# A two-layer graph-attention kernel on one core: weighing in column tiles of 32, single weight sums, and another order of the first step's loads and casts

## The chip, the core and the metric

The kernel runs on one core of a Trainium2 chip. Its time is the device time of one execution in microseconds (us). A profiled execution of each kernel is there too; its span, from the first to the last instruction, is a little shorter than the time of a run. The engines are TensorE (PE, with its weight loads shown apart as PEld), VectorE (DVE), ScalarE (ACT), GpSimd (POOL) and SyncE (SP, which here only issues DMAs; a queue's issue of a DMA is shown as SPq or ACTq).

## What is computed

64 graphs of 256 nodes with 512 features go through two layers of masked attention. `adj` says for each graph which node may look at which.

```python
# layer 0: 4 heads of 64, layer 1: 8 heads of 64
h = maximum(layernorm(x), 0)
q, k, v = heads(h @ Wq), heads(h @ Wk), heads(h @ Wv)
sim = where(adj, q @ k.T / 8, -big)
x = x + (softmax(sim) @ v) @ Wo + bo
# layer 1: the same on the new x, with a second layernorm (gamma, beta) behind the
# maximum, w_qkv and w_out in place of the four weights, and the diagonal always allowed
```

All arithmetic is on 32-bit floats.

## The kernel before

Two graphs make a step (`G = 2`), so that there are 32 steps. Everything of a step lies in SBUF: 128 partitions, and 512 tokens in four tiles of 128 (`NT = 4`). The order of the instructions on PE, DVE, ACT and POOL is written out by hand: `at(period, place, fn, ...)` puts each piece of work into a list with a due place, `place` being counted from the start of a period of 6.13 places, and at the end the list is sorted and each piece issued. One period is one step of the pipeline: layer 1 of step s, with layer 0 of steps s+1 and s+2 between its pieces. The place decides the order of issue on every engine, and each engine works strictly in that order.

The dense products (projections `project_qk`, `project_v1`, and the output product `combine1`) are done with a scheme of seven block products in place of eight (`PRODUCT`); for it, sums and differences of blocks of the weights and of the activations are made beforehand. `weight_sums` makes the four for the weights, `act_sums0` and `act_sums1` those for the activations. A set of seven products (`at_set`) takes one place, each product a seventh. PSUM has four banks for them; the results are taken out by `evacuate` on DVE and ACT.

Between the sets stand the visits of the attention (`visit`), six in a period, each for a pair of heads in two graphs. A visit does, for the pair of the visit before, `weigh` (values times probabilities, L823), then the sums of the probabilities by a matmul with ones (L843), and then the `scores` of the next pair (L787). In `weigh`, po is a PSUM tile of 128 partitions: the first head of the pair writes partitions 0 to 63, the second 64 to 127. There are eight matmuls in a visit's `weigh`, each with a stationary operand of 128 x 64 and 256 moving columns; two of them, one for each head, stand in different columns of the array. The matmuls with ones have a stationary operand of 128 x 32, and four of them stand beside one another. The scores have 64 rows and 128 columns, two beside one another. Each of these 32-bit matmuls is two records in the trace.

Behind the matmuls of a visit, `invert` (DVE, L853) makes the reciprocals of the sums, eight small DMAs on SP spread them over the partitions (`invb`), and `normalise` (POOL, L870) multiplies the weighed values with them. The probabilities of the next pair go from the scores through `mask_scores` (DVE, L800), `exponentials` (ACT, L805) and `key_halves` (POOL, L813). In the first layer POOL also multiplies the queries of each pair by a row `ne` (L699, in `project_qk` after products 3 and 4); the scores of a pair wait for that.

Before the first period a prologue loads and prepares. SP issues the loads of x in four pieces and of the adjacency matrix (`load_h`); ACT's queue issues those of the first layer's weights and the biases (`first_weights`). POOL casts the adjacency matrix (`adjacency_cast`, L502), then makes the row scales of the first layernorm (`row_scales`, L548 to L552), with which ACT and DVE scale x (`scale_row`). PE then transposes x (L608). The weights of the second layer are transposed on PE in 16 blocks (`weight_block`, L461), in gaps of the prologue; then `second_sums` makes the four sums of each of q, k and v on DVE and of the output weights on POOL. The sixteen are issued in four groups of four, one group directly after another on its engine.

Of the kernel before, what the change touches and what calls it, by code (L numbers as in the profile page):

```python
# [13 lines left out]
ALU = mybir.AluOpType  # L14
# [301 lines left out]
def fast_path(  # L316
# [19 lines left out]
    nc = tc.nc  # L336
    P = 128
    B, N, D = x.shape
    DH = 64
    G = 2  # L340
    NSTEP = B // G
    NIC = N // P
# [20 lines left out]
    def mm_tile(shape, dt=FP, hold=False):  # L363
        tag = next(b for b in banks if b not in held)
        banks.remove(tag)
        banks.append(tag)
        if hold:
            held.add(tag)
        return ps_mm.tile(shape, dt, name="mm", tag=tag)
# [26 lines left out]
    B_OF = ((0, 8, 7), (1, 3, 1))  # L396
    PRODUCT = {1: (0, 0), 2: (1, 1), 3: (6, 2), 4: (3, 6), 5: (2, 3), 6: (4, 4), 7: (5, 5)}

    def weight_sums(eng, w):
        eng.tensor_tensor(w[:, 5], w[:, 0], w[:, 2], ALU.subtract)  # L400
        eng.tensor_tensor(w[:, 2], w[:, 2], w[:, 3], ALU.add)
        eng.tensor_tensor(w[:, 4], w[:, 2], w[:, 0], ALU.subtract)
        eng.tensor_tensor(w[:, 6], w[:, 1], w[:, 4], ALU.subtract)

    def act_sums0(b, eng=nc.gpsimd):
        eng.tensor_tensor(b[:, 3], b[:, 7], b[:, 0], ALU.subtract)
# [9 lines left out]
    wqk0 = const.tile([P, NB, HC, 2, H0], FP, name="wqk0")  # L416
    wv0 = const.tile([P, NC, I0], FP, name="wv0")
    wo0 = const.tile([P, PR0, D], FP, name="wo0")
    wqkv1 = const.tile([P, NB, HC, 3, H1], FP, name="wqkv1")
    wo1 = const.tile([P, NB, HP1, HD], FP, name="wo1")  # L420
# [4 lines left out]
    def first_weights():  # L425
        for i in range(2):
            for k, w in enumerate((wq, wk)):
                nc.scalar.dma_start(
                    wqk0[:, 2 * i:2 * i + 2, :, k, :].rearrange("p j c o -> p (j c) o"),
                    w[:, i * H0:(i + 1) * H0].rearrange("(c p) o -> p c o", p=P),  # L430
                )
        nc.scalar.dma_start(wv0, wv.rearrange("(c p) o -> p c o", p=P))
        nc.scalar.dma_start(wo0, wo.rearrange("(c p) o -> p c o", p=P))
        for v, t in ((bo, bo_b), (b_out, bout_b)):
            nc.scalar.dma_start(t, bass.AP(tensor=v.tensor, offset=v.offset, ap=[[0, P], [1, D]]))
        gbr = sm.tile([2 * NC, P], FP, name="gbr", tag="inv", bufs=1)
        nc.scalar.dma_start(gbr[:NC], gamma.rearrange("(c p) -> c p", p=P))
        nc.scalar.dma_start(gbr[NC:], beta.rearrange("(c p) -> c p", p=P))
        return gbr
# [18 lines left out]
    def weight_block(wr, n, c):  # L458
# [3 lines left out]
        for i in range(2):  # L462
# [1 line left out]
            dst = wqkv1[:, blk, c % HC, n, :] if n < 3 else wo1[:, blk, c % HC, :]  # L464
            copy = nc.vector.tensor_copy if i == 0 and c % 2 == 0 else nc.scalar.copy
            copy(dst, pw[:, i * H1:(i + 1) * H1])

    def second_sums(k):
        if k == 3:
            weight_sums(nc.gpsimd, wo1)  # L470
        else:
            weight_sums(nc.vector, wqkv1[:, :, :, k, :])


    S = [dict() for _ in range(NSTEP)]
# [339 lines left out]
    def weigh(s, lyr, pr, first):  # L815
        st = S[s]
        p, pd = st.pop(("p", lyr, pr))
        po = ps_sc.tile([P, G, N], FP, name="sc")
        for g in range(G):
            for kc in range(NIC):  # L820
                for e in range(2):
                    c0 = pr * P + e * DH
                    nc.tensor.matmul(  # L823
                        po[e * DH:(e + 1) * DH, g, :],
                        st[f"v{lyr}"][:, g * NIC + kc, c0:c0 + DH],
                        p[e][:, g, kc, :], start=(kc == 0), stop=(kc == NIC - 1),
                    )
        if lyr == 0:
            if first:
                st["oT0"] = act.tile([P, PR0, G, N], FP, name="oT0")  # L830
            dst = st["oT0"][:, pr]
        else:
            if first:
                st["oT1"] = act.tile([P, NB + 1, HP1, N], FP, name="oT1")
            b0, b1, step = B_OF[pr // HP1]
            dst = st["oT1"][:, b0:b1:step, pr % HP1, :]
        nc.scalar.copy(dst, po)  # L837

        sums = mm_tile([P, N])
        for g in range(G):  # L840
            for e in range(2):
                r0 = 32 * (2 * g + e)
                nc.tensor.matmul(  # L843
                    sums[r0:r0 + 32, :], ones, pd[:, e, g, :], start=True, stop=True
                )
        st["dst", lyr, pr] = dst, sums
# [33 lines left out]
    def at(period, place, fn, *args):  # L880
        events.append((period * PERIOD + place, len(events), fn, args))
# [14 lines left out]
    def visit(period, w, prev, cur):  # L896

        w -= 0.0003
        if 0 <= prev[0] < NSTEP:
            at(period, w, weigh, *prev)  # L900
            last = prev[:2] == (NSTEP - 1, 1)
            at(period, w + (0.05 if last and prev[2] in (1, 3) else 0), invert, *prev[:3])
            at(period, w + 0.55, normalise, *prev[:3])
        if 0 <= cur[0] < NSTEP:
            at(period, w, scores, *cur)
            at(period, w, mask_scores, *cur, 0)
            at(period, w + 0.05, exponentials, *cur, 0)
            at(period, w + 1 / 7, mask_scores, *cur, 1)
            at(period, w + 0.18, exponentials, *cur, 1)
            at(period, w + 0.2, key_halves, *cur, 0)  # L910
            at(period, w + 0.3, key_halves, *cur, 1)

    AT_C0, AT_Q0, AT_V0, AT_H1, AT_C1 = 3.0, 3.57, 4.57, 5.13, 5.131
    for s in range(-1, NSTEP):
        p = s
# [14 lines left out]
    for s in range(NSTEP):  # L930

        p = s - 2
        if s == 1:
            p -= 3.93 / PERIOD
        at(p - 1 if s != 1 else -2, 5.7 if s != 1 else 3.2, load_h, s)
        at(p, 0.2 if s != 1 else 2.4, adjacency_cast, s)
        for t in range(NT):
            at(p, 0.5 + 0.4 * t if s != 1 else 1.8 + 0.2 * t, norm0, s, t)
            at(p, 2.3 + 0.1 * t if s != 1 else 2.6 + 0.1 * t, scale_row, s, t)
        at(p, (3.146, 3.584)[s] if s < 2 else 2.2, adjacency_turn, s)  # L940
        at(p, (3.3, 3.727)[s] if s < 2 else 2.75, masks, s)
        for c in range(NC):
            at(p, AT_C0 + 0.14 * (c // 2) + 0.001 * c, transpose_h, s, 0, c)
        at(p, AT_C0 + 0.1, lambda s=s: act_sums0(S[s]["hT"]))
        at(p, AT_C0 + 0.2, lambda s=s: act_sums1(S[s]["hT"]))
        at_set(p, AT_Q0 if s != 1 else 3.3, SET, project_qk, s, 0, 0)
        for t in range(NT):
            at_dense(p, AT_V0 + 0.14 * t, 0.14, project_v0, s, t)
        p = s - 1
        if s == 0:  # L950
            p -= 2.23 / PERIOD
        at(p, 1.0 if s else 0.0, load_x, s)
        at(p, 1.8 if s else 0.8, first_bias, s)
        for t in range(NT):
            at_dense(p, AT_C0 + 0.01 + 0.14 * t, 0.14, combine0, s, t)
            at(p, AT_C0 + 0.3 + 0.14 * t, norm1, s, t)
            at(p, (3.55, 3.7, 4.05, 4.2)[t], norm1_rest, s, t)
            at(p, 3.62 + 0.08 * t, second_bias, s, t)
            at(p, 4.5 + 0.1 * t, scale_row, s, t)

        for c in range(NC):
            at(p, AT_H1 + 0.0001 * c, transpose_h, s, 1, c)
        at(p, AT_C1 + 0.15, lambda s=s: act_sums0(S[s]["hT"]))
        at(p, AT_C1 + 0.5, lambda s=s: act_sums1(S[s]["hT"]))
        p = s
        at_set(p, 0.0, SET, project_qk, s, 1, 0)
        at_set(p, 1.0, SET, project_v1, s)
        at_set(p, 2.0, SET, project_qk, s, 1, 1)
        at(p, 4.55, lambda s=s: act_sums0(S[s]["oT1"], engine_of(s, 1, 1)))
        if s < NSTEP - 1:  # L970
            at(p, AT_C1 + 0.1, lambda s=s: act_sums1(S[s]["oT1"]))
            at_set(p, AT_C1, SETC, combine1, s)
            at(p, 6.3, store, s)
        else:
            at(p, AT_C1 + 0.4, lambda s=s: act_sums1(S[s]["oT1"], nc.vector))
            at_set(p, AT_C1, (1, 5, 2, 3, 6, 7, 4), combine1, s)
            for n, (i, j) in enumerate(((0, 0), (0, 1), (1, 1), (1, 0))):
                at(p, AT_C1 + (3, 6, 6, 7)[n] / 7, store_block, s, i, j)

    gbr, blocks = [], []  # L980
    at(-3, 5.71, lambda: gbr.append(first_weights()))
    at(-2, 2.25, lambda: weight_sums(nc.vector, wqk0))
    at(-2, 3.5, lambda: blocks.extend(weight_loads()))
    at(-2, AT_V0 + 0.2, lambda: gamma_beta(gbr[0]))
    for i in range(16):
        place = 3.3 - 3.93 + 1 / 7 - 0.0005 if i < 4 else 0.2 + 0.07 * i if i < 8 else 1.34 + 0.1 * (i - 8)
        at(-1, place, lambda i=i: weight_block(blocks[i // 4], i // 4, i % 4))
    for k, place in enumerate((2.8, 2.85, 4.3, 4.5)):
        at(-1, place, second_sums, k)
    for _, _, fn, args in sorted(events, key=lambda e: e[:2]):  # L990
        fn(*args)

# [51 lines left out]
```

## Time and profile before

| | before |
|---|---|
| three runs, us | 3487.59, 3490.94, 3491.87 (median 3490.94) |
| profiled execution: time, span in us | 3486.23, 3484.4 |
| granted TensorE clock, mean | 0.996 |
| busy: PE, PEld | 3422.2 us (98%), 2635.1 us (76%) |
| busy: DVE, POOL, ACT | 1926.1 us (55%), 1922.1 us (55%), 1245.8 us (36%) |
| DMA | mean 48 GB/s |
| PE busy from 0 to 200 us, 200 to 3300, 3300 to 3485 | 164.28, 3094.66, 163.31 us |

A line of the list of groups gives the kernel line, engine, operation, the tiles written and read, the shapes and the number of instructions, then the busy time and the mean duration. A busy time is the time in which at least one instruction of the group was under way, so that matmuls that stand beside one another count once. In a timeline the first number is the start in us from the beginning of the span, the second the length of a merged stretch, xN the number of instructions in it, and the bracket the idle time before it and who ended it. The ends of matmuls are modelled: their starts are what can be read closely.

### The profile page before, as it was taken

To read this page: it belongs to the slowest core of one execution; us is meant where nothing else is said; L and a number is where in the kernel's file an instruction comes from. 1 tells how busy PE (TensorE), PEld (TensorE's weight loads), DVE (VectorE), ACT (ScalarE), POOL (GpSimd) and SP (SyncE) were. 2 spreads that over 40 slices of the span, in tenths; PEclk is the share of its full clock that TensorE was granted. 3 is DMA by queue.
4 is the path that set the end of the run, shared out by engine and by line. 5 is a ranking of instruction groups with operands and counts; after the bars stand their busy time and mean duration, and the time that the engine had idled before them with its cause. 6 is when DMAs were issued, how large, how long until landed. Compare 5 with 4: busy or idle time off the path is not lost.

```text
span 3484.4 us, 52897 instructions
## 1 busy us (share of the span) xinstructions
PE 3422.2 (98%) x19586; PEld 2635.1 (76%) x19586; DVE 1926.1 (55%) x3410; ACT 1245.8 (36%) x2197; POOL 1922.1 (55%) x1790
## 2 busy tenths in 40 slices
PE   7899999999999999999999999999999999999998
PEld 5677777877777777778777777777777777777766
DVE  4755565555565555655555655556555556555554
ACT  3333333333333333333343333333333333333331
POOL 4565655556555656555565556565556555555641
PEclk9999999999999999999999999999999999999999
DMA  3111011111111110111111111101111111111011
GB/s 126 37 53 53 28 43 52 54 54 31 51 42 53 53 52 28 44 51 54 54 40 41 42 54 53 52 27 45 51 54 54 42 40 42 54 54 51 14 42 38
DMA packets 147513, 165.57 MB, mean 48 GB/s; under 512 B 43304, under 2 KB 96048, under 8 KB 147248
## 3 DMA queue, kind: packets, MB, share of 16 engines
q1 hardware_dynamic: 141728, 155.16, 14.6%
q10 hardware_dynamic: 5520, 6.95, 0.6%
q8 instruction: 157, 2.57, 0.3%
q14 instruction: 108, 0.88, 0.1%
HBM read 78.12 MB, written 33.55 MB: 32 GB/s over the span
## 4 chain that ended last, share of the span: by engine, by line
PE 87%; POOL 6%; issue 5%; DVE 1%; ACT 0%; DMA 0%; SPq 0%; POOLq 0%; ACTq 0%; DVEq 0%
PE mm L689 26%; PE mm L730 11%; PE mm L755 11%; PE sc L787 10%; PE sc L823 8%; PE mm L716 6%; PE mm L741 6%; PE mm L608 3%; PE mm L843 3%; POOL pd L813 1%; POOL qk L699 1%; POOL oT L870 1%; POOL r L548 1%; POOL xt L588 1%; PE mm L510 0%
## 5 line engine op out<-in xcount | busy, mean ns | idle before, releaser
L813 POOL TENSOR_TENSOR pd<-p 128x512 f32<-128x512 f32 x380 | 478.1, 1273 | 830.1 <-ACT p L805 712.8
L689 PE MATMUL mm<-hT,wqkv 128*128 128x256 f32 x3584 | 804.4, 382 | 10.3 <-ACT qk L623 10.1
L689 PEld LDWEIGHTS mm<-hT,wqkv 128*128 128x128 f32 x3584 | 674.5, 190 | 122.9 <-issue 20.9
L805 ACT ACTIVATE p<-p 128x512 f32<-128x512 f32 x768 | 458.9, 629 | 496.5 <-DVE p L800 495.3
L853 DVE RECIPROCAL inv<-mm 128x128 f32<-128x128 f32 x384 | 339.8, 926 | 365.5 <-PE mm L843 347.5
L800 DVE TENSOR_TENSOR p<-sc,n 128x512 f32<-128x512 f32 x768 | 481.1, 682 | 3.7 <-PE sc L787 3.7
L837 ACT COPY oT<-sc 128x512 f32<-128x512 f32 x192 | 112.5, 586 | 1019.5 <-PE sc L823 1019.4
L689 PE MATMUL mm<-hT,wqk 128*128 128x256 f32 x1792 | 401.6, 381 | 2.5 <-ACT hT L612 1.0
L755 PE MATMUL mm<-wo,oT 128*128 128x256 f32 x1792 | 395.6, 381 | 4.9 <-DVE oT L870 3.3
L730 PE MATMUL mm<-wqkv,hT 128*128 128x256 f32 x1792 | 395.3, 381 | 0.0
L689 PEld LDWEIGHTS mm<-hT,wqk 128*128 128x128 f32 x1792 | 337.4, 190 | 71.7 <-DVE inv L853 9.9
L787 PE MATMUL sc<-qk 64*128 64x256 f32 x3072 | 384.2, 389 | 7.2 <-POOL qk L699 6.0
L823 PE MATMUL sc<-p,v 128*64 128x256 f32 x3072 | 378.3, 387 | 5.1 <-ACT p L805 5.1
L730 PEld LDWEIGHTS mm<-wqkv,hT 128*128 128x128 f32 x1792 | 337.8, 190 | 55.2 <-issue 10.6
L755 PEld LDWEIGHTS mm<-wo,oT 128*128 128x128 f32 x1792 | 339.5, 191 | 52.0 <-DVE oT L870 4.1
L787 PEld LDWEIGHTS sc<-qk 64*128 64x128 f32 x3072 | 281.2, 186 | 114.1 <-issue 65.8
L823 PEld LDWEIGHTS sc<-p,v 128*64 128x64 f32 x3072 | 205.3, 137 | 154.8 <-issue 62.4
L870 POOL TENSOR_TENSOR oT<-oT,invb 128x512 f32<-128x512 f32 x190 | 241.7, 1272 | 93.9 <-DMA invb<-inv 86.1
L657 POOL TENSOR_TENSOR xt<-xt,u 128x512 f32<-128x512 f32 x93 | 118.0, 1269 | 257.9 <-DVE xt L650 188.4
L559 ACT ACTIVATE h<-h,mr,r 128x512 f32<-128x512 f32 x252 | 197.4, 808 | 123.7 <-POOL mr L552 123.7
L646 DVE TENSOR_TENSOR xt<-mm,xt 128x512 f32<-128x512 f32 x64 | 44.2, 691 | 336.8 <-PE mm L755 336.8
L741 PE MATMUL mm<-wo,oT 128*128 128x512 f32 x512 | 230.4, 593 | 0.0
(112 smaller groups left out, 3797.0 us busy)
## 6 DMA issues: line engine op xcount, KB each, us to landing
invb<-inv SPq DMA_DIRECT2D x1532, 32.0 KB, 1.8
xt<-in_x_dram SPq DMA_DIRECT2D x32, 1024.0 KB, 5.1
h<-in_x_dram SPq DMA_DIRECT2D x31, 1024.0 KB, 5.1
out_dram<-xt SPq DMA_DIRECT2D x31, 1024.0 KB, 4.7
ad<-in_adj_dram SPq DMA_DIRECT2D x32, 128.0 KB, 4.4
wr<-in_L_gnn_w_qkv_dram ACTq DMA_DIRECT2D x3, 1024.0 KB, 12.4
h<-in_x_dram SPq DMA_DIRECT2D x4, 256.0 KB, 3.5
wr<-in_L_gnn_w_out_dram ACTq DMA_DIRECT2D x1, 1024.0 KB, 16.2
```

Source lines behind the costliest of these rows:

```text
L689: nc.tensor.matmul(bank[:, k, :], w[:, wa, c, k, a * P:(a + 1) * P], st["hT"][:, ba, c, :], start=first and (k, c) == (0, 0), stop=(k, c) ...
L716: nc.tensor.matmul(bank, st["hT"][:, b0 + t // NIC * step, c % HC, i:i + P], wv0[:, c, :], start=(c == 0), stop=(c == NC - 1),)
L730: nc.tensor.matmul(bank[:, t, :], st["hT"][:, ba, c, t * P:(t + 1) * P], wqkv1[:, wa, c, 2, :], start=first and (t, c) == (0, 0), stop=(t, ...
L741: nc.tensor.matmul(bank, st["oT0"][:, pr, t // NIC, t % NIC * P:(t % NIC + 1) * P], wo0[:, pr, :], start=(pr == 0), stop=(pr == PR0 - 1),)
L755: nc.tensor.matmul(bank[:, t, :], st["oT1"][:, ba, c, t * P:(t + 1) * P], wo1[:, wa, c, :], start=first and (t, c) == (0, 0), stop=(t, c) ...
L787: nc.tensor.matmul(sc[g][e][:, kc, :], qk[rows, 1, k0:k0 + P], qk[rows, 0, g * N:(g + 1) * N], start=True, stop=True,)
L800: nc.vector.tensor_tensor(p[e][:, g], sc[e], neg[:, :, g, :], ALU.add)
L805: nc.scalar.activation(p[e][:, g], p[e][:, g], AF.Exp, scale=SCALE)
L813: engine_of(s, lyr, pr).tensor_tensor(pd[:, e], p[e][:, :, 0, :], p[e][:, :, 1, :], ALU.add)
L823: nc.tensor.matmul(po[e * DH:(e + 1) * DH, g, :], st[f"v{lyr}"][:, g * NIC + kc, c0:c0 + DH], p[e][:, g, kc, :], start=(kc == 0), stop=(kc ...
L853: nc.vector.reciprocal(inv[:, i * P:(i + 1) * P], sums[:, i * P:(i + 1) * P])
L870: engine_of(s, lyr, pr).tensor_tensor(dst, dst, invb, ALU.mult)
```

## The change

The change has four parts.

First, `weigh` makes sixteen matmuls of 32 columns in place of eight of 64: each head's 64 values are cut into two tiles of 32, and four matmuls with the same place in the accumulation stand in four column tiles of the array.

Second, the sums of the weights become single pieces of work with places of their own (`weight_sum`). Those of layer 1's q and k are put earlier, into the prologue of the first steps; those of v stand in the first period between the pieces there, and those of the output weights on POOL likewise.

Third, the first layer's weights and biases are loaded by SP's queue, behind x and the adjacency matrix, and no longer by ACT's. The cast of the first step's adjacency matrix is put behind its row scales on POOL, and the sums of the first layer's weights behind the scaling of x on DVE.

Fourth, the `normalise` of pair 1 of layer 1 moves from 0.55 to 0.63 places behind its visit. That visit is at place 3.857, the third product of the set beside it gives its result to POOL at 4.43: POOL's multiplication by `ne` (L699) for product 3 now stands ahead of that `normalise` (L870), where it stood behind it.

```diff
-    def weight_sums(eng, w):
-        eng.tensor_tensor(w[:, 5], w[:, 0], w[:, 2], ALU.subtract)
-        eng.tensor_tensor(w[:, 2], w[:, 2], w[:, 3], ALU.add)
-        eng.tensor_tensor(w[:, 4], w[:, 2], w[:, 0], ALU.subtract)
-        eng.tensor_tensor(w[:, 6], w[:, 1], w[:, 4], ALU.subtract)
+    def weight_sum(eng, w, i):
+
+        n, a, b, op = (
+            (5, 0, 2, ALU.subtract), (2, 2, 3, ALU.add), (4, 2, 0, ALU.subtract), (6, 1, 4, ALU.subtract),
+        )[i]
+        eng.tensor_tensor(w[:, n], w[:, a], w[:, b], op)
...
     def first_weights():
         for i in range(2):
             for k, w in enumerate((wq, wk)):
-                nc.scalar.dma_start(
+                nc.sync.dma_start(
...
-        nc.scalar.dma_start(wv0, wv.rearrange("(c p) o -> p c o", p=P))
-        nc.scalar.dma_start(wo0, wo.rearrange("(c p) o -> p c o", p=P))
+        nc.sync.dma_start(wv0, wv.rearrange("(c p) o -> p c o", p=P))
+        nc.sync.dma_start(wo0, wo.rearrange("(c p) o -> p c o", p=P))
         for v, t in ((bo, bo_b), (b_out, bout_b)):
-            nc.scalar.dma_start(t, bass.AP(tensor=v.tensor, offset=v.offset, ap=[[0, P], [1, D]]))
+            nc.sync.dma_start(t, bass.AP(tensor=v.tensor, offset=v.offset, ap=[[0, P], [1, D]]))
...
-    def second_sums(k):
-        if k == 3:
-            weight_sums(nc.gpsimd, wo1)
-        else:
-            weight_sums(nc.vector, wqkv1[:, :, :, k, :])
...
         for g in range(G):
             for kc in range(NIC):
-                for e in range(2):
-                    c0 = pr * P + e * DH
+                for r0 in range(0, P, 32):
                     nc.tensor.matmul(
-                        po[e * DH:(e + 1) * DH, g, :],
-                        st[f"v{lyr}"][:, g * NIC + kc, c0:c0 + DH],
-                        p[e][:, g, kc, :], start=(kc == 0), stop=(kc == NIC - 1),
+                        po[r0:r0 + 32, g, :],
+                        st[f"v{lyr}"][:, g * NIC + kc, pr * P + r0:pr * P + r0 + 32],
+                        p[r0 // DH][:, g, kc, :], start=(kc == 0), stop=(kc == NIC - 1),
                     )
...
-            at(period, w + 0.55, normalise, *prev[:3])
+            at(period, w + (0.63 if prev[1:3] == (1, 1) else 0.55), normalise, *prev[:3])
...
-        at(p, 0.2 if s != 1 else 2.4, adjacency_cast, s)
+        at(p, (2.9, 2.4)[s] if s < 2 else 0.2, adjacency_cast, s)
...
-    at(-2, 2.25, lambda: weight_sums(nc.vector, wqk0))
+    for i in range(4):
+        at(-2, 2.75, weight_sum, nc.vector, wqk0, i)
...
-    for k, place in enumerate((2.8, 2.85, 4.3, 4.5)):
-        at(-1, place, second_sums, k)
+    for i in range(4):
+        at(-1, 0.1 + 0.01 * i, weight_sum, nc.vector, wqkv1[:, :, :, 0, :], i)
+        at(-1, 1.0 + 0.01 * i, weight_sum, nc.vector, wqkv1[:, :, :, 1, :], i)
+        at(0, 0.2 + i / 7, weight_sum, nc.vector, wqkv1[:, :, :, 2, :], i)
+        at(0, 1.3 + 0.5 * i, weight_sum, nc.gpsimd, wo1, i)
```

## The prediction

> **What bounds the kernel now.** I read the shares of busy time first, then PE's waits, then timelines of PE and its neighbours. PE is busy for 98% of the span, and the chain that ended last is PE's by 87%. So what counts is how long PE's own stream is, and the few places where it stands still. PE's waits, longest first, in total, times and longest:
>
> ```profile
> PE mm L608 <- ACT h L559: 22.0, 7, 15.4
> PE mm L689 <- ACT qk L623: 10.8, 2, 10.1
> PE sc L787 <- POOL qk L699: 6.0, 31, 0.5
> PE sc L823 <- ACT p L805: 5.1, 4, 1.7
> ```
>
> Three of the four parts of the change touch one of the first three lines each: the first wait of 15.4 us is the start of the program, the 10.1 us is a single hole, and the third comes back once a period.
>
> A visit in the middle (timeline of PE, then of POOL):
>
> ```profile
> 1577.59 1.95 PE L823 MATMUL sc<-p,v 128*64 128x256 f32 x16
> 1579.46 0.64 PE L843 MATMUL mm<-pd,ones 128*32 128x256 f32 x8
> 1580.26 2.00 PE L787 MATMUL sc<-qk 64*128 64x256 f32 x16 [0.16 <-POOL qk L699]
> ```
> ```profile
> 1577.70 1.28 POOL L870 TENSOR_TENSOR oT<-oT,invb 128x512 f32<-128x512 f32 x1
> 1578.94 1.27 POOL L699 TENSOR_TENSOR qk<-qk,ne 128x512 f32<-128x512 f32 x1
> ```
>
> Weighing takes 1.87 us until the sums start. Listed record by record, a visit's starts are the same all over the span. The last dense matmul starts 0.309 us ahead of the weighing, although dense matmuls follow one another at 0.2157 us. The 16 records of weighing go in 8 steps of two column tiles (7 ns apart); the first step takes 0.267 us, the others 0.2157, so 1.568 us from first to last start. Then 0.309 us to the sums, whose two steps of four tiles (each 6.6 ns behind the last) are 0.240 us apart, 0.260 us from first to last start; then 0.309 us to the scores, in all 2.447 us. The same 93 ns over a step (0.309 - 0.216) stand wherever the array's division changes (64*128 to 128*128: 0.306), and nowhere where it stays: L716 to L741 0.216, L522 to L689 0.216, L608 to L741 0.109 after steps of 0.109.
>
> The hole, and what DVE did ahead of it:
>
> ```profile
> 122.64 8.99 PE L689 MATMUL mm<-hT,wqkv 128*128 128x256 f32 x32 [10.09 <-ACT qk L623]
> ```
> ```profile
> 99.85 0.68 DVE L400 TENSOR_TENSOR wqkv<-wqkv 128x512 f32<-128x512 f32 x1
> ...
> 116.36 1.63 DVE L403 TENSOR_TENSOR wqkv<-wqkv 128x512 f32<-128x512 f32 x1
> 117.92 1.76 DVE L853 RECIPROCAL inv<-mm 128x128 f32<-128x128 f32 x2
> ...
> 120.17 2.48 DVE L800 TENSOR_TENSOR p<-sc,n 128x512 f32<-128x512 f32 x4
> ```
>
> Twelve sums hold DVE for 18 us. The reciprocal and the masks are queued behind them, although their sums and scores were there by 106.6; ACT's exponentials wait for the masks, the copy that frees product 1's bank stands behind two of the exponentials on ACT, and PE has no bank.
>
> The start, from POOL's timeline: the cast waits for the adjacency matrix and holds the row scales behind it.
>
> ```profile
> 10.66 1.14 POOL L502 CAST adb<-ad 128x1024 bf16<-128x1024 uint8 x1 [9.35 <-DMA ad<-in_adj_dram]
> 11.88 0.51 POOL L568 TENSOR_SCALAR ve<-mv 128x4 f32<-128x4 f32 x1
> ...
> 14.30 0.20 POOL L552 TENSOR_TENSOR mr<-mr,r 128x4 f32<-128x4 f32 x1
> ```
>
> **What the Trainium skill says.** "TensorEngine Tiling (Array Packing)", Key Properties: "Changing tiling mode (not just tile) drains the TensorE". The trace agrees: 93 ns at each change. "DMA: Bandwidth & Descriptors", Queues, rings and completion order: SP and ACT each have one ring on each of the same 16 DMA engines, taken in ring order; so loads on two queues interleave, and on one queue the later ones come behind. The trace fits: x's four pieces were ready for DVE only at 3.67, 5.39, 6.98 and 8.24 us, while ACT's weights were on their way. "GPSIMD Engine Reference", Specifications: its SBUF interfaces are shared with VectorE, with contention when a DVE instruction has two SBUF inputs. The trace agrees: the sums above took 0.69 us with POOL idle and 1.64 with it busy, and POOL's operations of 1.27 us took 1.6 to 1.7.
>
> **The change part by part.**
>
> *Weighing.* What goes is one change of division: weighing and sums are both 128*32 afterwards. The stream keeps 8 steps, each with four tiles instead of two, since four tiles go side by side in the sums as two do here. A visit then has 32 records of matmul and 32 of weight load in place of 16 and 16, 6144 more PE instructions in all. New visit: first step 0.240 (the one of the sums, with loads of 32 columns), six steps of 0.2157, so the last step starts at 1.534; the first of the sums one plain step later, since their weights can be loaded ahead, at 1.750; their second step at 1.966, last tile 0.020 later, 1.986; scores 0.309 later, 2.295. Saved: 2.447 - 2.295 = 0.152 us a visit. Of 192 visits some 186 are in a stream that PE sets (not three in the prologue, whose ends others set, and three at the end, which wait for ACT): 186 x 0.152 = 28.3 us. Bounds: if the drain stays, only the first step's 0.027 us is saved, 5 us; if entering the weighing gets cheaper as well, some 10 us more.
>
> *Normalise.* L699 needs DVE's result (1576.66 here) and the row scales before it on POOL (until 1577.57). It then ends near 1578.9, not 1580.2, and the scores can start at 1579.8, so that the wait goes even with PE 0.15 us earlier. The start of the sums' last record to the scores is 0.538 to 0.557 us in these visits, against 0.309: 31 x 0.236 = 7.3 us. L870 moves to L699's old place; what waits for it, L406, still starts after both. Bounds 5 and 7.5.
>
> *Start.* Without the cast, the row scales start when DVE has the moments: at 9.2 us as now, or earlier since x no longer shares the DMA engines. A whole x of 1 MB lands in 5.1 us in the steady part; DVE needs 0.87 us for each of four pieces from 3.67 on, so 7.1 us is the earliest. From there 2.62 us on POOL and 0.9 on ACT: PE starts between 12.7 and 10.6, against 15.40. I take 4.5 us saved, bounds 2.5 and 5. The cast (ready by 12) is still ahead of its transposes, 16 of x coming first. SP's eight moved issues, 0.35 to 0.67 us each on ACT, stand ahead of the second step's adjacency load, which waits for the cast anyway, and so delay nobody; the weights should land by 13 us, their sums (0.69 us each) end by 16, and the first product that needs one starts near 19. ACT loses eight issues that no one waited for. All later waits of the prologue hang on this chain and move with it.
>
> *Sums.* In the order of DVE the q sums fall between L629 and L633 near 70 us, the k sums between two L745 near 81, in idle times of 1.29 and 2.75 us: 4 x 0.69 = 2.8 us, POOL being idle. The first delay L633 and the banks behind it by about 0.45 us, as L635 now follows at 73.5 instead of 73.05; the second nobody. Then the reciprocal starts at 104.5, the masks end at 109.4, ACT's copy near 109.3, before product 6 and 5 are through at 111.8: the hole of 10.09 us and the wait of 0.22 close. The v sums stand singly between L625, L627 and L629; with POOL busy at 1.64 us each they can hold the seventh product's bank, 0 to 1.9 us on PE, I take 0.8. The four POOL sums (1.27 us each) fall into idle times of POOL of 5.75 and 11.49 us. Saved: 10.3 - 0.45 - 0.8 = 9.0 us; bounds 5 (all sums at 1.64) and 10.3.
>
> Sum: 28.3 + 7.3 + 4.5 + 9.0 = 49.1 us, on the profiled span 3484.4 to 3435.3. The runs' median is 6.5 us above that span; taken off the median, 3490.9 - 49.1 = 3441.8 us.
>
> **The rivals.** *The drain stays* (chance 0.14). The 93 ns may belong to the change of operands or PSUM tile between L823 and L843, not to the division. Then 5 + 20.8 = 26 us, 3465. Against: other borders between tiles at one division show none. No border between two four-tile streams is in the trace, so it can't be excluded.
>
> *PE's instruction supply becomes the bound* (0.07), the case on the other side. Weighing and sums need 80 instructions in 2 us. The sequencer's record of a wait ahead of L843 starts 0.02 us after the weighing's first load, 32 instructions ahead of what executes, so 48 must be delivered meanwhile. The densest stretch before (32, 16 and 32 in 4.1 us) shows only that supply is under 85 ns each. At 62 ns each, the figure of "TensorE: Matmul & The Clock Gate", Back-to-back issue gap, for a MATMUL decoded in software (for the loads too, my guess), a visit would take 3.0 + 0.3 us: 0.84 more, 186 x 0.84 = 156 us against 20.8 saved elsewhere, 3626. It decides from 47 ns each: 48 x 0.047 = 2.25 us is where a visit costs what the other parts save. Against: the sums' 16 records start within 0.26 us and the scores behind them come without a gap, so supply is not near its limit there; how near is not shown.
>
> *Waits take the gain* (0.06): PE comes earlier and meets POOL or DVE. POOL and DVE have 45% idle and after L699 no wait of each period is left, so little speaks for it; half of the weighing's gain lost gives 3456. That the change doesn't act at all is excluded, as the order of instructions shows each part.
>
> **How the numbers follow.** The main case has 0.73; its own range, with its bounds (5 + 5 + 2.5 + 28 to 38 + 7.5 + 5 + 10), is 3430 to 3450. To 8 in 10 it reaches up to the drain's case: 3431 to 3466. A measurement of this kernel can tell about 0.2%, 7 us, from no change. Faster by more than that are the main case, the drain's, the waits', 0.93, with a little off for small gains: 0.92; same 0.02; slower 0.06.
>
> **What would show it.** Right: 2.3 us from the start of weighing to that of the scores, and no 93 ns between weighing and sums; no line L787 waiting for L699; PE's first matmul at 10.6 to 12.7; no hole near 110 us. Wrong: steps of weighing over 0.216 us, or a new wait of PE in each period.

## The result and the profile after

| | before | after |
|---|---|---|
| median of the runs beside one another, us | 3491.12 (3487.59 to 3491.87, 4 runs) | 3434.41 (3433.67 to 3435.47, 4 runs) |
| span of the profiled execution, us | 3484.4 | 3433.7 |
| busy PE, PEld, us | 3422.2, 2635.1 | 3391.8, 2632.4 |
| chain that ended last: PE, POOL, issue | 87%, 6%, 5% | 97%, 1%, 0% |

The ratio is 0.984, with a 95% interval of 0.9823 to 0.9857. The spans differ by 50.7 us where the sum of the prediction said 49.1; the medians differ by 56.7, because the span of before's profiled execution lay 6.7 us under the median of its runs and that of after only 0.7 us under its own. In a second comparison the changed kernel had 3436.55 us (3435.02 to 3437.01, 4 runs) against 3486.51, ratio 0.9856 (0.9839 to 0.9872): 50.0 us. Unless said otherwise, "after" below is the first comparison's profiled execution, "the second execution of after" that of the other, and a median is compared with that of the runs of before beside it.

PE's waits after (engine, tile and line that wait, releaser: total us, times, longest):

```profile
PE mm L603 <- ACT h L554: 15.9, 7, 10.2
PE sc L817 <- ACT p L800: 5.2, 4, 1.7
PE mm L750 <- DVE oT L864: 3.4, 2, 2.6
...
PE mm L684 <- ACT qk L618: 1.5, 1, 1.5
...
PE sc L782 <- POOL qk L694: 0.5, 1, 0.5
```

The kernel's line numbers are now 5 or 6 less. The start went from 15.4 to 10.2 us, the hole of 10.1 us is gone (what stands as L684 waiting for ACT's copies is a wait of 1.5 us near 23 us), and of the 31 waits of the scores for POOL one is left, which stood in the prologue before as well. Here is an early visit of the kind that waited, in PE's timeline:

```profile
177.80 1.93 PE L817 MATMUL sc<-p,v 128*32 128x256 f32 x32
179.56 0.61 PE L837 MATMUL mm<-pd,ones 128*32 128x256 f32 x8
180.10 2.00 PE L782 MATMUL sc<-qk 64*128 64x256 f32 x16
```

From the start of the weighing to the scores it is 177.80 to 180.10, 2.30 us, and no bracket stands behind the scores. Record by record: 1.555 us from the weighing's first to its last start, 0.196 to the sums, 0.236 for them, 0.309 to the scores, together 2.296. (The step into the weighing stays at 0.309.) The step to the sums is measured from the last of four tiles, which starts 20 ns behind the first; inside the weighing the step from a last tile to the next first is 0.196 too. So nothing is paid any more at this border. The place where the hole was, in PE's timeline:

```profile
102.07 12.35 PE L684 MATMUL mm<-hT,wqkv 128*128 128x256 f32 x56
114.36 1.93 PE L817 MATMUL sc<-p,v 128*32 128x256 f32 x32
```

All 56 records of the set stand in one stretch; before they were in three, over 24.95 us from 106.61 to the weighing at 131.56, now 12.29. DVE at that time, and POOL at the start (two timelines):

```profile
100.28 1.77 DVE L847 RECIPROCAL inv<-mm 128x128 f32<-128x128 f32 x2 [4.06 <-PE mm L837]
102.55 2.48 DVE L795 TENSOR_TENSOR p<-sc,n 128x512 f32<-128x512 f32 x4
104.94 0.68 DVE L404 TENSOR_TENSOR wqkv<-wqkv 128x512 f32<-128x512 f32 x1
105.90 0.69 DVE L620 TENSOR_TENSOR qk<-mm,qk 128x512 f32<-128x512 f32 x1 [0.28 <-PE mm L684]
```
```profile
7.41 0.19 POOL L563 TENSOR_SCALAR ve<-mv 128x4 f32<-128x4 f32 x1 [6.10 <-DVE mv L536]
...
9.06 0.20 POOL L547 TENSOR_TENSOR mr<-mr,r 128x4 f32<-128x4 f32 x1
9.20 1.04 POOL L497 CAST adb<-ad 128x1024 bf16<-128x1024 uint8 x1
```

The reciprocal waits for PE alone, the masks follow it, and a single sum of weights slips in between two evacuations. On POOL the row scales start with the moments at 7.41 us and the cast comes behind them.

So the 50.7 us fall into three stretches, read from the starts of named matmuls. Up to the first weighing behind the hole (131.56, now 114.36) it is 17.2 us. From there to the last record of the sums (3457.7, now 3405.4) it is 35.1. The rest of the span became longer, 26.7 to 28.3 us: minus 1.6. In the second execution of after the three are 15.2, 35.7 and 0.3.

### The profile page after: what moved, and what is told of

The parts are those of the page before. It is cut to its first block, busy times and chain, and to the rows that moved or that the text cites. A ratio compares the mean times of both kernels' runs of the same rounds, so it can differ in the third digit from the quotient of the medians.

```text
span 3433.7 us, 59040 instructions
## 1 busy us (share of the span) xinstructions
PE 3391.8 (99%) x22658; PEld 2632.4 (77%) x22658; DVE 1916.3 (56%) x3410; ACT 1245.3 (36%) x2197; POOL 1919.4 (56%) x1790
## 3 DMA queue, kind: packets, MB, share of 16 engines
q1 hardware_dynamic: 144928, 157.79, 15.4%
## 4 chain that ended last, share of the span: by engine, by line
PE 97%; DVE 1%; POOL 1%; ACT 0%; issue 0%; DMA 0%; ACTq 0%; SPq 0%; DVEq 0%; POOLq 0%
PE mm L684 34%; PE mm L725 11%; PE mm L750 11%; PE sc L782 10%; PE sc L817 10%; PE mm L711 6%; PE mm L736 6%; PE mm L603 3%; PE mm L837 2%; PE mm L505 0%; PE mm L517 0%; DVE inv L847 0%; DVE bs L535 0%; SPq L859 0%; ACTq L456 0%
## 5 line engine op out<-in xcount | busy, mean ns | idle before, releaser
L684 PE MATMUL mm<-hT,wqkv 128*128 128x256 f32 x3584 | 802.0, 381 | 0.0
L684 PEld LDWEIGHTS mm<-hT,wqkv 128*128 128x128 f32 x3584 | 673.9, 190 | 111.0 <-issue 20.9
L684 PE MATMUL mm<-hT,wqk 128*128 128x256 f32 x1792 | 401.6, 381 | 3.4 <-ACT qk L618 1.5
L684 PEld LDWEIGHTS mm<-hT,wqk 128*128 128x128 f32 x1792 | 337.6, 190 | 72.3 <-DVE inv L847 9.9
L725 PEld LDWEIGHTS mm<-wqkv,hT 128*128 128x128 f32 x1792 | 338.0, 190 | 55.1 <-issue 10.6
L817 PE MATMUL sc<-p,v 128*32 128x256 f32 x6144 | 374.5, 382 | 5.2 <-ACT p L800 5.2
L817 PEld LDWEIGHTS sc<-p,v 128*32 128x32 f32 x6144 | 180.4, 109 | 171.0 <-issue 62.2
L711 PE MATMUL mm<-wv,hT 128*128 128x256 f32 x1024 | 230.3, 382 | 0.0
## 6 DMA issues: line engine op xcount, KB each, us to landing
wr<-in_L_gnn_w_qkv_dram ACTq DMA_DIRECT2D x3, 1024.0 KB, 13.5
```

The costliest lines, as they stand in the source:

```text
L684: nc.tensor.matmul(bank[:, k, :], w[:, wa, c, k, a * P:(a + 1) * P], st["hT"][:, ba, c, :], start=first and (k, c) == (0, 0), stop=(k, c) ...
L711: nc.tensor.matmul(bank, st["hT"][:, b0 + t // NIC * step, c % HC, i:i + P], wv0[:, c, :], start=(c == 0), stop=(c == NC - 1),)
L725: nc.tensor.matmul(bank[:, t, :], st["hT"][:, ba, c, t * P:(t + 1) * P], wqkv1[:, wa, c, 2, :], start=first and (t, c) == (0, 0), stop=(t, ...
L817: nc.tensor.matmul(po[r0:r0 + 32, g, :], st[f"v{lyr}"][:, g * NIC + kc, pr * P + r0:pr * P + r0 + 32], p[r0 // DH][:, g, kc, :], start=(kc ...
```

## The experiments

Each edit is made to the kernel before, unless the text says that it is made to the changed one.

**The parts one by one.** The first four kernels each do one part alone. If the theory holds, their gains add up to the whole, and each shows in its own view.

```diff
-                for e in range(2):
-                    c0 = pr * P + e * DH
+                for r0 in range(0, P, 32):
...
-                        po[e * DH:(e + 1) * DH, g, :],
+                        po[r0:r0 + 32, g, :],
...
```

> The first part alone: sixteen matmuls of 32 columns in weighing, all else as before. My theory (the gain is the drain at a change of the array's division): a visit takes 2.296 us from the start of weighing to the scores, as with the whole change, in five visits of six; in the sixth the scores still wait for POOL's multiplication, so the 0.152 us saved ahead of it become waiting. 186 x 0.152 - 31 x 0.152 = 23.6 us shorter than before. Rival (the visits gain in full whatever POOL does): 28 us. Rival (the gain of the visits comes only together with the other parts): under 10 us.

Measured: 3463.92 us (3462.67 to 3464.42) against 3488.14, 24.2 us less; ratio 0.9927 (0.9913 to 0.994). A visit takes 2.296 us, as in the whole change. But in the visit that waits for POOL the new time is not kept. PE's waits of this kernel:

```profile
PE sc L787 <- POOL qk L699: 10.9, 31, 0.6
```

It was 6.0 us before, for the same 31 waits: POOL comes when it came, PE comes 0.15 us earlier and waits for that much longer. That is 4.9 us of the weighing's gain that only the fourth part releases.

```diff
-            at(period, w + 0.55, normalise, *prev[:3])
+            at(period, w + (0.63 if prev[1:3] == (1, 1) else 0.55), normalise, *prev[:3])
```

> The fourth part alone: normalise of pair 1 behind the multiplication by ne on POOL. My theory: the wait of the scores for POOL goes in 31 visits, 0.236 us each, 7.3 us shorter than before, and nothing takes its place. Rival: the operations moved behind it are then waited for (the output products or the second multiplication), and the time stays within 2 us of before.

Measured: 3480.95 us (3478.7 to 3484.81), 7.2 less; ratio 0.9978 (0.9969 to 0.9988). PE's waits, two of its lines:

```profile
PE mm L689 <- ACT qk L623: 8.1, 1, 8.1
...
PE sc L787 <- POOL qk L699: 0.5, 1, 0.5
```

This wait has gone from 31 times to one; the hole of the prologue is still there, with 8.1 us in this execution. The interval of the ratio allows 4 to 11 us, so that the medians alone do not fix the 7.2; the record of the visits does: from the sums' last start to the scores these 30 visits took 0.54 us before, and take 0.309 here.

The third kernel has only the second part, for layer 1's weights:

```diff
...
-    for k, place in enumerate((2.8, 2.85, 4.3, 4.5)):
-        at(-1, place, second_sums, k)
+    for i in range(4):
+        at(-1, 0.1 + 0.01 * i, weight_sum, nc.vector, wqkv1[:, :, :, 0, :], i)
+        at(-1, 1.0 + 0.01 * i, weight_sum, nc.vector, wqkv1[:, :, :, 1, :], i)
+        at(0, 0.2 + i / 7, weight_sum, nc.vector, wqkv1[:, :, :, 2, :], i)
+        at(0, 1.3 + 0.5 * i, weight_sum, nc.gpsimd, wo1, i)
```

> The second part alone, without the sums of the first layer's weights: the sums of layer 1's weights one by one at their new places. My theory: the hole of 10.09 us on PE goes, and with it what the hole costs behind its end: the traces show 24.95 us from the first matmul of the set to the next weighing before and 12.29 after the whole change. I put the rest, about 1.9 us, down to a lower granted TensorE clock behind the hole (0.78 and 0.81 before, 1.00 after the change). So 12.7 us shorter than before, with the clock at 1.00 from 107 to 132 us. Rival (the 1.9 us belong to waits that another part takes away): 10.3 to 11 us shorter, and the stretch of 32 records behind the third product stays at 8.9 us instead of 7.

Measured: 3476.37 us (3473.91 to 3477.95), 11.8 less; ratio 0.9962 (0.9948 to 0.9975). The set stands closed from 107.64 to 119.92. From its start to the next weighing that is 12.28 us in place of 24.95, and more is gone than the two idle times of 10.09 and 0.22 us. The windows tell where most of the rest is. First before, then this kernel; the columns are the stretch, its length, the busy us and instructions of PE, PEld, DVE, ACT and POOL, the granted clock, the DMA share and GB/s:

```profile
107.00:123.00 16.00, 5.69 (x25) 4.39 (x24) 15.62 (x16) 2.11 (x4) 10.21 (x7) 0.78 0.03 8
123.00:132.00 9.00, 9.00 (x36) 7.28 (x37) 4.28 (x9) 1.22 (x3) 4.70 (x4) 0.81 0.12 30
```
```profile
107.00:123.00 16.00, 16.00 (x94) 12.65 (x92) 11.82 (x21) 3.92 (x7) 8.76 (x7) 1.00 0.17 49
123.00:132.00 9.00, 9.00 (x50) 7.67 (x47) 7.05 (x14) 3.24 (x6) 4.00 (x4) 1.00 0.13 31
```

Before, PE is busy for all of 123 to 132 us and does only 36 matmuls in it, at a mean clock of 0.81; here it does 50 at 1.00. The hole had cost its own length and then slow matmuls: the set's last 32 records took 8.99 us where 32 records of the same form in a stretch take 7.17. The Trainium skill tells this in "TensorE: Matmul & The Clock Gate", What's actually happening: after an idle window of about 3.4 us the clock falls to half, and a busy one brings it back. The records of the clock agree: half from 116.1 us on, 3.6 us after PE's last matmul had ended, for 10.2 us, so until 3.7 us after PE had started again at 122.64.

The fourth kernel has the third part: the eight loads go from `nc.scalar.dma_start` to `nc.sync.dma_start`, and

```diff
-        at(p, 0.2 if s != 1 else 2.4, adjacency_cast, s)
+        at(p, (2.9, 2.4)[s] if s < 2 else 0.2, adjacency_cast, s)
...
-    at(-2, 2.25, lambda: weight_sums(nc.vector, wqk0))
+    at(-2, 2.75, lambda: weight_sums(nc.vector, wqk0))
```

> The third part alone: weights on SP's queue behind x and the adjacency matrix, the first cast behind the row scales, the first layer's weight sums behind the scaling. My theory: PE's first matmul starts near 10.2 us instead of 15.4, and 4.5 to 5 us of it are still there at the end of the program. Rival (the later waits of the prologue hang on other loads and swallow it): the start is earlier but less than 2 us remain at the first dense set of layer 1.

Measured: 3481.53 us (3480.43 to 3483.93), 6.6 less; ratio 0.9981 (0.9973 to 0.9989). PE starts at 10.49 us in place of 15.40, and 5.1 us of it are left at the weighing behind the hole (126.44, not 131.56).

The four add up to 24.2 + 7.2 + 11.8 + 6.6 = 49.8 us, each known to some 3 to 5 us by its interval. With the 4.9 us that the weighing wins in the waiting visits once the fourth part is there, it is 54.7, between the 50.0 and 56.7 us by which the whole was faster. The next kernel asks for that interaction from the other side: the changed kernel with `normalise` back at 0.55.

> The whole change but the fourth part: normalise of pair 1 back at 0.55 places. My theory: the scores of one visit in six wait for POOL again, now for the old 0.236 us and for the 0.152 us by which weighing ends earlier: 31 x 0.388 = 12 us longer than the changed kernel, 44.7 us shorter than the kernel before by medians. Rival (parts simply add): 7.3 us longer than the changed kernel, 49.4 us shorter than before.

Measured: 3446.37 us (3444.92 to 3450.53), 40.0 under the before beside it, ratio 0.9885 (0.9869 to 0.9902). Against after's two medians, which were not taken beside it, that is 12.0 and 9.8 us more, by spans 11.3 and 11.8. The 44.7 and 49.4 us of the two cases were taken from the first comparison's 56.7; from the second's 50.0 they would be 38.0 and 42.7, and 40.0 lies between them. So the medians do not decide. PE's waits, and the scores of the visit shown above, now with their wait:

```profile
PE sc L782 <- POOL qk L694: 10.3, 31, 0.5
```
```profile
183.30 2.00 PE L782 MATMUL sc<-qk 64*128 64x256 f32 x16 [0.33 <-POOL qk L694]
```

The record of the visits decides: 30 of them take 0.71 us from the sums' last start to the scores, where after has 0.309 in each; that is 11.9 us in all. The same edit that gives 7.2 us alone gives some 12 behind the others: in each of these visits the 0.236 us of the prediction and about the 0.152 us of the weighing.

**Loads or order?** The third part has two halves, and the prediction let them act together. Two kernels, each run once, ask which half does what; beside them before had a span of 3486.4. The first has only the two places of the diff above, with the loads left on ACT.

> From the third part the order on POOL and DVE alone: the cast behind the row scales, the weight sums behind the scaling, loads on ACT's queue as before. Theory that the order on POOL is what counts: the row scales start at 9.2 us, when the moments are ready as before, and PE's first matmul at 12.5 to 12.8 us instead of 15.4, over half of the 5.2 us. Theory that the loads count: it starts at 15 or later.

Measured: PE starts at 12.74 us, 2.66 earlier than before; span 3483.2, 3.2 less. The second has only the loads on SP and the later sums, with the cast first.

> From the third part the loads alone: weights on SP's queue behind x and the adjacency matrix, the cast ahead of the row scales as before, the weight sums behind the scaling. Theory that the loads count: the moments are ready near 7.3 us, the adjacency matrix lands near 7 too, no longer sharing the DMA engines, and PE starts at 10.5 to 11.5 us. Theory that the order on POOL counts: the cast still waits until about 10 us, and PE starts at 13.5 to 15.

Measured: PE starts at 11.65, 3.75 earlier; span 3481.3, 5.1 less. POOL's timeline of each, one line:

```profile
9.26 0.19 POOL L568 TENSOR_SCALAR ve<-mv 128x4 f32<-128x4 f32 x1 [7.95 <-DVE mv L541]
```
```profile
7.76 1.04 POOL L502 CAST adb<-ad 128x1024 bf16<-128x1024 uint8 x1 [6.46 <-DMA ad<-in_adj_dram]
```

In the first, POOL still waits for the moments until 9.26, since x arrives as late as before. In the second the cast has its matrix at 7.76 in place of 10.66, and the row scales behind it start at 8.89 in place of 11.88. Together the halves give 4.9 us (15.40 to 10.49, the third part alone; in two executions of after 10.16 and 10.51) and not 2.66 + 3.75 = 6.4: once the loads have gone, there is less that the cast holds up.

**Does the division of the array make the drain, or is it the 32 columns?** If the drain of 93 ns belongs to the change of division, sums with 64 columns should spare it behind a weighing with 64 columns too. The sums' ones become a pair of 128 x 64, each with ones in the half of its head and zeros in the other; the two heads are accumulated, so that the sums come out in the same rows.

```diff
...
-        for g in range(G):
-            for e in range(2):
-                r0 = 32 * (2 * g + e)
+        for e in range(2):
+            for g in range(G):
                 nc.tensor.matmul(
-                    sums[r0:r0 + 32, :], ones, pd[:, e, g, :], start=True, stop=True
+                    sums[64 * g:64 * g + 64, :], ones[:, e, :], pd[:, e, g, :],
+                    start=(e == 0), stop=(e == 1),
                 )
```

> The kernel before, with weighing in column tiles of 64 as before, and the sums of the probabilities also in tiles of 64 columns: two tiles side by side, each adding two matmuls whose stationary operands have ones in one half and zeros in the other, with the same results. Theory that equal division spares the drain: from the last record of weighing to the first of the sums 0.20 to 0.22 us instead of 0.309, though no tile is 32 wide; the sums take 0.65 us instead of 0.26 from first to last start, the visit 2.73 us, and the span is about 45 us longer than before. Rival (tiles of 32 or four side by side are what spares it): 0.309 us stay, the visit takes 2.84 us, the span is about 66 us longer.

Measured: span 3533.7, 47.3 more than the one of before beside it (3486.4) and 49.3 more than the one of the table; the run took 3535.61 us. A visit in PE's timeline:

```profile
1599.37 1.95 PE L825 MATMUL sc<-p,v 128*64 128x256 f32 x16
1601.15 1.03 PE L844 MATMUL mm<-pd,ones 128*64 128x256 f32 x8
1602.11 2.00 PE L789 MATMUL sc<-qk 64*128 64x256 f32 x16
```

The kernel is slower because the sums now have four steps, not two. But from the last start of the weighing to the first of the sums it is 0.209 us where it was 0.309, and 0.209 is also what a step inside the weighing takes from a last tile to the next first: an equal division spares the drain, whichever it is. The Trainium skill's sentence in "TensorEngine Tiling (Array Packing)", Key Properties, that the mode and not the tile decides, is what both kernels show.

**How near is PE's instruction supply to its limit?** The changed kernel, with 96 matmuls of 128 x 32 by 16 moving columns put at its very start, where PE has nothing to do:

```diff
+        for _ in range(24):
+            for r0 in range(0, P, 32):
+                nc.tensor.matmul(
+                    bank[r0:r0 + 32, :16], ones, ones[:, :16], start=True, stop=True
+                )
...
```

> The changed kernel with 96 small matmuls more at the very start, before PE has anything to do: stationary 128 x 32, 16 moving columns, four column tiles, results unused; 192 records of matmul and 192 of weight load. They need little time in the array, so past the first 32 instructions their pace is that of PE's instruction supply. The losing rival of the prediction needed more than 47 ns per instruction. If supply is as fast as the changed kernel's visits demand, under 27 ns each, all 384 take less than 10.4 us; at 31 ns (62 a pair) 12 us; at 62 ns 24 us.

Measured, PE's timeline:

```profile
2.08 2.76 PE L978 MATMUL mm<-ones 128*32 128x16 f32 x192 [2.08 <-DVE ones L380]
```

192 records of matmul and as many of weight load stand in 2.76 us; each 32 instructions take 0.213 us, 6.7 ns for one, from the first to the last. The losing case needed 47 ns, seven times as much. Span 3433.0: at the start they cost nothing. This is one burst of 384 instructions; that supply holds over the whole run is shown by the visits of after, which stay at 2.296 us.

**A wait that grew.** ACT has a load of 1 MB (`w_out`) in its queue ahead of its first copies. In the changed kernel this issue lasts from 16.82 to 22.26 us, and PE waits 1.50 us for the copy behind it, which runs at 22.31; before it was 0.69 us. ACT and its queue in before, then in after (the list puts ACT's idle time down to PE, whose product was there long before):

```profile
22.28 4.81 ACTq L455 DMA_DIRECT2D wr<-in_L_gnn_w_out_dram  x1
27.13 0.59 ACT L623 COPY qk<-mm 128x512 f32<-128x512 f32 x1 [5.87 <-PE mm L689]
```
```profile
16.82 5.44 ACTq L456 DMA_DIRECT2D wr<-in_L_gnn_w_out_dram  x1
22.31 0.58 ACT L618 COPY qk<-mm 128x512 f32<-128x512 f32 x1 [6.69 <-PE mm L684]
```

With the third part alone the wait is only 0.51 us: there the issue lasts 4.58 us, until 22.06, and PE comes to its first dense set at 16.89, 0.8 us later than in after. PE's lead over the kernel before is, in after, 5.64 us at the start of the first dense set (16.10 against 21.74) and 4.82 behind this wait (22.95 against 27.77). The load was first put on SP's queue:

```diff
-            nc.scalar.dma_start(wr, src[r0 * P:(r0 + 4) * P].rearrange("(r p) i -> p r i", p=P))
+            queue = nc.scalar if n < 3 else nc.sync
+            queue.dma_start(wr, src[r0 * P:(r0 + 4) * P].rearrange("(r p) i -> p r i", p=P))
```

> The changed kernel, with the load of the output weights of layer 1 issued by SP instead of ACT. In the changed kernel ACT's queue is held by the issue of that load until 22.26 us, and the copy behind it on ACT, which PE waits 1.50 us for, comes late. My theory: PE's wait at 22.95 us goes and the span is 1 to 1.5 us shorter than the changed kernel's 3433.7. Rival (SP is then held as long, and the load of x for the residual behind it comes late): the wait moves to POOL's bias additions near 36 us, and the span is unchanged or longer.

Measured: 3439.09 us (3438.1 to 3439.55), ratio 0.9862 (0.9845 to 0.9878), and a span 3.3 us longer than after's: a miss. The wait for ACT is gone, but PE's waits have a new line:

```profile
PE mm L685 <- DVE qk L625: 5.1, 1, 5.1
```

In DVE's timeline, a little before that evacuation (L625, at 31.59):

```profile
29.97 0.70 DVE L536 BATCH_NORM_STATS2 bs<-h 128x6 f32<-128x512 f32 x1 [6.41 <-DMA h<-in_x_dram]
```

DVE waits until 29.97 us for the next step's x, and an evacuation that PE needs is queued behind that. SP now issues the load at 9.17 us and the residual's x at 11.12, both ahead of the next step's x at 14.62; in after the next step's x went out at 14.14, ahead of the residual's at 14.57. Which of the two loads ahead holds it up was not tried apart. So the load stayed on ACT in the next kernel, but is issued behind the first copy:

```diff
+            load = lambda wr=wr, src=src, r0=r0: nc.scalar.dma_start(
+                wr, src[r0 * P:(r0 + 4) * P].rearrange("(r p) i -> p r i", p=P)
+            )
...
+    at(-2, 3.72, lambda: at_late[0]())
```

> The changed kernel, with the load of layer 1's output weights still on ACT's queue, but issued behind the copy of the first product instead of ahead of it; SP's order stays. Theory (that copy, held behind the blocked issue, is what PE waits 1.50 us for, and nothing on SP moves): the wait goes, the second batch of products starts near 21.4 us instead of 22.95, and 1 to 1.5 us remain of it in the span. Rival (the loads themselves, 4 MB and x at once, set the pace): the issue blocks ACT in its new place and the next copy comes late, PE waits there and the span is unchanged.

Measured: 3435.94 us (3430.64 to 3437.51), ratio 0.9855 (0.9838 to 0.9871), beside 3436.55 for the changed kernel as it is, run once more:

> The changed kernel once more, beside the one with the later load and on the same chip: a span of 3432 to 3434 us and a median 52 to 57 us under that of the kernel before.

In PE's timeline of the late load the wait has closed:

```profile
16.08 12.25 PE L690 MATMUL mm<-hT,wqk 128*128 128x256 f32 x56
28.80 2.00 PE L788 MATMUL sc<-qk 64*128 64x256 f32 x16 [0.47 <-POOL qk L700]
```

The scores start at 28.80 where they started at 30.59. The span of this execution, 3428.9, is 4.3 us under that of after beside it, more than the wait was; it also has no half clock in the prologue. By medians the two kernels are 0.6 us apart, inside the 6.9 us over which the runs of the late load spread: whether it is worth anything over the whole kernel is not settled.

## Why the prediction was right, step by step

*Weighing.* Right in the sum, 2.296 us a visit against 2.295, and in its terms: counted from the start of the weighing, as there, its last step starts at 1.535 us for 1.534, the sums at 1.751 for 1.750, their second step at 1.967 for 1.966. With *normalise* it was to give 35.6 us; between the first weighing behind the hole and the last sums the two executions gave 35.1 and 35.7. By medians, each alone gave 24.2 and 7.2 us. The prediction had put the whole 28.3 under the weighing, with the 31 waiting visits; alone the weighing doesn't have these, since the scores waited for POOL. That the fourth part must come with it was in the text ("the wait goes even with PE 0.15 us earlier"), and the two kernels show it.

*Normalise.* 7.3 us predicted, 7.2 measured alone, within a wide interval. One of the 31 visits counted is in the prologue, and its wait stays.

*Start.* PE was to start at 12.7 to 10.6 us and started at 10.16, in the second execution at 10.51, so 4.9 to 5.2 us earlier where 4.5 were taken. At the set where the hole was PE was 4.5 us ahead of before (102.07 against 106.61), in the second execution only 2.5 (104.09): what is left there goes with the half clock ahead of it, one piece of 3.4 us in the first and two in the second, and that it is just the 4.5 in the first is chance. The earliest time for POOL was put at 7.1; it is 7.41. "All later waits of the prologue hang on this chain and move with it" failed in one place: the wait for ACT's copy at 22.95 us grew from 0.69 to 1.50, since the issue of a load ahead of it lasted longer, 5.44 us and not 4.81. The order on POOL is worth 2.66 us alone and 1.2 behind the loads (11.65 to 10.49).

*Sums.* This is the term that was mis-sized: 9.0 us predicted, with the cost of the q sums taken off, and 12.4 measured: 12.7 from the set's start to the next weighing (24.95 to 12.29), less 0.3 for the q sums. Most of what was taken off was not there. The q sums cost 0.28 us, not 0.45: from the last transposes of weights ahead of layer 0's v to the second group of v's matmuls it is 3.47 us before (72.85 to 76.32) and 3.75 with the second part alone (73.81 to 77.56) as in the changed kernel (67.89 to 71.64). The v sums took 0.68, 0.89, 0.68 and 0.94 us, though POOL was at work beside three of them, not the 1.64 of the sums before, and no product of the set waits for its bank: their 0.8 us did not come. And 2.3 us were missing from the sum. The part of the set that PE did at half clock behind the hole is 1.8 of them; the other 0.5 are the two stops, since the list counts a wait only from the modelled end of the last matmul, 0.27 us later than the next could have started. The length of a wait in the list is not its whole price.

*The end.* The sum has nothing for it. In the first execution of after, the last stretch grew by 1.6 us. PE's timeline there, after and then the second execution of after:

```profile
3416.44 8.43 PE L750 MATMUL mm<-wo,oT 128*128 128x256 f32 x30 [0.78 <-DVE oT L864]
```
```profile
3417.81 6.74 PE L750 MATMUL mm<-wo,oT 128*128 128x256 f32 x30 [0.78 <-DVE oT L864]
```

The same 30 matmuls take 8.43 us and 6.74: again the granted clock. The first execution has it at half from 3416.97 to 3420.39 us, within this stretch; the second from 3410.86 to 3414.27, ahead of it.

*The sum against the median.* 49.1 us were taken off a span and off a median alike, though the profiled execution of before lay 6.5 us under that median. This offset belonged to the runs of before in the first comparison, and not to the kernel: in three later comparisons their median was 3488.14, 3486.42 and 3486.51. The forecast of 3441.8 us is 7.4 over the measured 3434.41 for that reason above all; as a span, 3435.3 was 1.6 over. That it came so near is in part luck: by stretches of the first execution it is 17.2 us up to the first weighing behind the hole where 4.5 + 9.0 = 13.5 were taken, 35.1 for the 35.6 of *weighing* and *normalise* behind it, and minus 1.6 at the end for nothing, so that the error of the sums was taken back in part by the other two. In the second execution the first stretch gave 15.2.

*The rivals.* The drain that stays is refuted by 0.196 us and by the 0.209 of the sums with 64 columns. The supply as the bound is refuted by 6.7 ns and by the visits of 2.296 us. That waits take the gain is true of the weighing alone in one visit of six, and of no visit of the whole change behind the prologue.

## What to carry to other kernels

Where groups of small matmuls follow one another, cut them so that neighbours share the division of the array: each border that went gave back some 0.1 us. It pays only where no group needs more steps for it: the sums with 64 columns gave back 0.10 us and cost 0.39. When an engine's stream gets shorter, look at the waits that stand in it: one of 0.16 us in one visit of six takes the whole gain of that visit, unless what it waits for is moved too. And price a long hole of PE by what follows it as well, and a moved load by the engine whose queue its issue holds.

## What the runs showed of the hardware

- Between two groups of matmuls with the same division of the array, the step is the same as inside a group: from the last tile to the next first 0.196 us with four tiles of 32 columns, 0.209 with two of 64, at the border as within. Where the division changes it is 0.309 or 0.306 us at every border in the middle of before and after.
- Half clock comes in the prologue and at the end in pieces of 3.4 us, or a few of them together, that lie elsewhere in each execution of the same kernel. In the prologue: one at 89.0 us in the first of after, two at 89.7 and 96.5 in the second, none in the profiled one of the late load. In the 3.4 us ahead of these three PE was busy for 1.4 to 1.8. How much of the spread between runs they make is not shown.
- One DMA of 1 MB, issued on ACT behind three others, held ACT for 4.81 us before, 5.44 and 5.80 in the two executions of after, 6.15 with `normalise` back at 0.55, 4.58 with the third part alone and 4.05 in the late load's kernel; the three ahead took 1.80 to 2.24 us together. Except in the late load's kernel, the copy behind it on ACT, for which PE waited, ran only after it. What sets the length is open.
